# Layer 1 of a four-layer graph kernel: one fp32r product of 256 columns for two weights, and a new order of the work around it

## The chip, the cores and the metric

The kernel runs on one core of a Trainium2 chip. The core has five engines with queues of their own: TensorE (PE; its weight loads are shown as PEld), VectorE (DVE), ScalarE (ACT), GpSimd (POOL) and SyncE (SP), which here only issues DMAs. The metric is device time in microseconds of one execution; it stands at 913.17 us before the change, the median of 3 runs (912.57 to 913.24).

## The reference, cut to what matters

Four residual layers work on x, 32 samples of 512 tokens with 128 features, and share one 512 x 512 matrix adj. The change lies in layer 1, a Chebyshev graph convolution of order 2 whose two matrices are both adj:

```python
# h = max(layernorm(x), 0); A1 = A2 = adj
hops(h, A) = [h A, 2 (h A) A - h]          # A acts on the token axis
xs  = [h] + hops(h, adj) + hops(h, adj)
out = relu(concat(xs) @ Theta1 + bias)     # Theta1: 5 blocks of 128 x 128
x   = x + out
```

Since both matrices are adj, the five blocks of Theta1 fold into three: th[0] = T0 - T2 - T4 for h itself (the "own part"), th[1] = T1 + T3 for one hop, th[2] = 2 (T2 + T4) for two hops. With x1 = adj applied to h, the layer is h th[0] + adj (h th[1] + x1 th[2]) + bias, and then relu and the residual sum.

## The kernel before

All of x stays in SBUF. xt[q] holds a pair q of samples (q = 0 to 15, b = 0 or 1 in it), xq[r] a quadruple r (0 to 7). TensorE, DVE, ACT and POOL execute in the order of the source (manual_schedule, line 182), so the Python order of the calls is each engine's queue. SP is not in that list: its DMAs are placed by the framework, except where keep_in_program_order holds them.

Products with adj use three fp32r products instead of an fp32 one: an operand is split in parts high, low and mid (moving_parts, line 418: high on ACT, low on POOL, mid on DVE), and the three partial products with the parts of adj add up in one PSUM bank. Projections with the small weights are plain fp32 products of 128 columns (projected, line 442). A sample has four token tiles (NT = 4).

Layer 1 (layer1, line 950) runs a loop over r with the pairs A = 2r and C = 2r + 1. For each pair:

- normalised (line 956) makes h with eight ACT rows; turn (line 964) transposes it in 32 x 32 blocks on DVE and sends it through DRAM (four writes, then one read, on SP), so that h comes back with its features on the partitions, as hT.
- straighten (line 971) copies hT into the token order, hs, on POOL, two copies for a pair.
- split_up (line 976) splits a sample's h in its three parts; first (line 981, with mixed_parts, line 400) makes x1 transposed: 12 fp32r products of 512 columns, with one eviction on ACT (line 407).
- weighed (line 986) makes w = h th[1] + x1 th[2] in one bank, 8 fp32 products of 128 columns, and evicts it in three parts (lines 992 to 994: high on ACT, low and mid on DVE).
- mix (line 996) is called four times for a quadruple, one token tile i of all four samples each: four fp32 products of the own part, hs with th[0] (line 999), then 12 fp32r products of 512 columns with adj and w (line 1003). DVE then adds the bias and takes relu plus residual (lines 1005 and 1007).

In the loop, the mixing of quadruple r - 1 comes early in round r, between the preparations of pairs A and C. ln_stats and own take the layer-norm statistics of finished pairs for the next layer (four DVE rows, one ACT square root, two short DVE rows). The generator square, advanced by go(square, ...), prepares the square of adj for layer 2 on POOL, one step at a time in rounds 3 to 6. In the last round, more(0) to more(7) (line 1358) start layer 2.

The tiles that matter: small_tile, 13 of 128 x 512 (parts of h, x1, features); wide_tile, 6; the pool tag hT, 4 (hT and hs of pairs); 8 PSUM banks. A tile is taken again only after its last reader.

The weights of layer 1 are combined on POOL late in layer 0 (late_parts, line 733); line 744 scales th[0] by 1/UP, since mixing multiplies the whole bank by UP afterwards.

Of the kernel before, what the change touches and what calls it, by code (L numbers as in the profile page):

```python
# [9 lines left out]
F32 = mybir.dt.float32  # L10
# [4 lines left out]
OP = mybir.AluOpType  # L15
# [14 lines left out]
def kernel(  # L30
# [56 lines left out]
    def tiles(ap):  # L87
        return ap.rearrange("p (t f) -> p t f", f=D)

    def blk(t):  # L90
        return slice(t * P, (t + 1) * P)
# [56 lines left out]
    def spread(w, n):  # L148
        return w[:, None, :].to_broadcast([P, n, D])
# [250 lines left out]
    def mixed_parts(name, left, right, dst):  # L400

        p = bank(f"p_{name}")
        for part in range(3):
            for t in range(NT):
                nc.tensor.matmul(p, right[part][:, blk(t)], left[part][:, t, :],  # L405
                                 start=(t == 0 and part == 0), stop=(t == NT - 1 and part == 2))
        nc.scalar.activation(dst, p, AF.Copy, scale=UP)  # L407

    def three(name):
        return [small_tile(f"{part}_{name}", F32R) for part in PARTS]  # L410
# [7 lines left out]
    def moving_parts(x, high, low, mid):  # L418

        nc.scalar.activation(high, x, AF.Copy, scale=DOWN)  # L420
        nc.gpsimd.tensor_sub(low, x, high.bitcast(F32))  # L421
        nc.vector.scalar_tensor_tensor(mid, x, 1.0 / UP, high.bitcast(F32), OP.mult, OP.subtract)  # L422

    def scaled_parts(x_low, high, low, mid):

# [13 lines left out]
    def columns(xT):  # L439
        return lambda t: xT[:, blk(t)]  # L440

    def projected(name, *terms):

        p = bank(name)
        for t in range(NT):
            for i, (hT, w) in enumerate(terms):
                nc.tensor.matmul(p[:, blk(t)], hT(t), w, start=(i == 0),  # L447
                                 stop=(i == len(terms) - 1))
        return tiles(p)
# [283 lines left out]
    def late_parts():  # L733

        adj_parts.extend(matrix_tile(f"adj_{part}", F32R) for part in PARTS[:2])
        high, low = adj_parts
        for t in range(NT):
            nc.scalar.activation(high[:, t, :], adj_s[:, t, :], AF.Copy, scale=DOWN)
            tc.keep_in_program_order(nc.gpsimd.tensor_sub(adj_s[:, t, :], adj_s[:, t, :], high[:, t, :].bitcast(F32)))
            yield  # L740
        for out, op, p, q in ((1, OP.add, 1, 3), (2, OP.add, 2, 4), (0, OP.subtract, 0, 2)):
            tc.keep_in_program_order(nc.gpsimd.tensor_tensor(th[:, out, :], th[:, p, :], th[:, q, :], op))
        tc.keep_in_program_order(nc.gpsimd.tensor_scalar(th[:, 2, :], th[:, 2, :], 2.0, None, OP.mult))
        nc.gpsimd.tensor_scalar(th[:, 0, :], th[:, 0, :], 1.0 / UP, None, OP.mult)
        for t in range(NT):
            nc.scalar.activation(low[:, t, :], adj_s[:, t, :], AF.Copy, scale=LOW)
        yield
        adj_parts.append(matrix_tile(f"adj_{PARTS[2]}", F32R))
        for t in range(NT):
            tc.keep_in_program_order(nc.gpsimd.tensor_sub(adj_parts[2][:, t, :], high[:, t, :].bitcast(F32),  # L750
                                                          low[:, t, :].bitcast(F32)))
            yield
# [197 lines left out]
    def layer1(more, square):  # L950


        h, hT, hs, parts, x1, w = {}, {}, {}, {}, {}, {}
        normal, turning = {}, {}

        def normalised(q, n=2 * NT):
            if q >= NQ:
                return
            if q not in normal:
                h[q] = normed_tile(q)  # L960
                normal[q] = normed_steps(q, h[q])
            go(normal[q], n)

        def turn(q, n=3):
            if q >= NQ:
                return
            if q not in turning:
                turning[q] = turn_steps(h[q], f"hT1_{q}", hT)
            go(turning[q], n)

        def straighten(q):
            hs[q] = work.tile([P, 2, N], F32, tag="hT", name=f"hs_{q}", bufs=4)
            for b in range(2):
                nc.gpsimd.tensor_copy(split(hs[q][:, b]), hT[f"hT1_{q}"][:, :, b, :].rearrange("p b (a c) -> p a b c", c=QR))  # L974

        def split_up(q, b):
            if q < NQ:
                parts[q, b] = three(f"h_{q}_{b}")
                moving_parts(h[q][:, b].rearrange("p t f -> p (t f)"), *parts[q, b])

        def first(q, b):
            if q < NQ:
                x1[q, b] = small_tile(f"x1T_{q}_{b}")
                mixed_parts(f"x1T_{q}_{b}", adj_parts, parts[q, b], x1[q, b])

        def weighed(q, b):
            r, j = q // 2, 2 * (q % 2) + b
            if j == 0:
                w[r] = [wide_tile(f"w_{part}_{r}", F32R) for part in PARTS]
            p = projected(f"p_w_{q}_{b}", (columns(hs[q][:, b]), th[:, 1, :]), (columns(x1[q, b]), th[:, 2, :]))  # L990
            high, low, mid = (part.rearrange("p t (w f) -> p t w f", f=D)[:, :, j, :] for part in w[r])
            nc.scalar.activation(high, p, AF.Copy, scale=DOWN)
            nc.vector.tensor_sub(low, p, high.bitcast(F32))
            nc.vector.scalar_tensor_tensor(mid, p, 1.0 / UP, high.bitcast(F32), OP.mult, OP.subtract)

        def mix(r, i):
            p = bank(f"p_l1_{r}_{i}")
            for j in range(4):
                nc.tensor.matmul(p[:, blk(j)], columns(hs[2 * r + j // 2][:, j % 2])(i), th[:, 0, :],  # L999
                                 start=(j == 0), stop=False, skip_group_check=True)  # L1000
            for part in range(3):
                for t in range(NT):
                    nc.tensor.matmul(p, adj_parts[part][:, t, blk(i)], w[r][part][:, t, :],  # L1003
                                     start=False, stop=(part == 2 and t == NT - 1), skip_group_check=True)
            nc.vector.scalar_tensor_tensor(tiles(p), tiles(p), UP, spread(b1, 4), OP.mult, OP.add)
            x = xq[r].rearrange("p w b t f -> p (w b) t f")[:, :, i, :]
            nc.vector.scalar_tensor_tensor(x, tiles(p), 0.0, x, OP.max, OP.add)

        normalised(0)
        yield  # L1010
        turn(0)
        normalised(1)
        yield
        split_up(0, 0)
        split_up(0, 1)
        first(0, 0)
        straighten(0)
        turn(1)
        for r in range(NQ // 2):
            A, C = 2 * r, 2 * r + 1  # L1020
            last = r == NQ // 2 - 1
            if r == 0:
                first(A, 1)
                split_up(C, 0)
                split_up(C, 1)
                straighten(C)
            else:
                split_up(A, 1)
                straighten(A)
                mix(r - 1, 0)  # L1030
                normalised(C, NT)
                turn(C, 1)
                mix(r - 1, 1)
                normalised(C)
                turn(C)
                mix(r - 1, 2)
                split_up(C, 0)
                go(square, r > 3)
                mix(r - 1, 3)
                split_up(C, 1)  # L1040
                first(A, 1)
            weighed(A, 0)
            weighed(A, 1)
            if last:
                more(0)
            go(square, r > 2)
            first(C, 0)
            normalised(A + 2, NT)
            if last:
                more(1)  # L1050
            if r:
                ln_stats(A - 2)
            else:
                go(own[NQ - 3])
                go(own[NQ - 2])
            first(C, 1)
            if last:
                more(2)
            if r:
                straighten(C)  # L1060
            split_up(A + 2, 0)
            normalised(A + 2)
            go(square, r > 3)
            weighed(C, 0)
            weighed(C, 1)
            ln_stats(C - 2) if r else go(own[NQ - 1])
            go(square, r > 3)
            turn(A + 2)
            first(A + 2, 0)
            if r == 0:  # L1070
                normalised(C + 2, 0)
        more(3)
        for i in range(NT):
            mix(r, i)
            more(4 + i)
        yield
# [177 lines left out]
    def layers_2_and_3():  # L1254
# [15 lines left out]
        for n in range(B):  # L1270
# [16 lines left out]
                fetch(2, 2)  # L1287
            elif n % 2 and n + 5 < B:
                fetch(2, n // 2 + 3)
            if n in (2, 3):  # L1290
                ln_stats(NQ - 4 + n)
            if n == 12:
                weights_of_3()
            if n == 20:
# [135 lines left out]
```

## Time and profile before

| what | us |
|---|---|
| median of 3 runs | 913.17 |
| lowest, highest | 912.57, 913.24 |
| the profiled execution, its own time | 912.96 |
| its span on the core | 911.2 |
| layer 1 on TensorE, first product with adj to last mixing | 183.6 to 450.6 |

The page gives, for each engine, busy time and share of the span. A group line gives source line, engine, operation, output and inputs, shape, count, then the busy time in us with the mean of one row in ns, and the idle time before these rows with what ended it. A timeline line gives start, length, engine, line, operation and count; neighbouring rows of one kind are merged, so that its length runs from the first start to the last end. The chain of waits is followed back from the last instruction; in order of time, each piece is given with its start and length. In the view of stretches, each engine's busy time is followed by its number of rows, and the last three columns are TensorE's granted clock, the share of the DMA engines and their GB/s.

An fp32 product leaves two matmul records, an fp32r product one.

### The profile page before, as it was taken

The numbers are of one execution on the slowest core, as the hardware profiler recorded it, in microseconds if no ns is written. First come the engines' busy times: TensorE is split into PE (matmuls) and PEld (weight loads), VectorE is DVE, ScalarE is ACT, GpSimd is POOL, SyncE is SP. The second block draws the span as 40 slices with busy tenths as digits, with TensorE's granted clock in tenths as the row PEclk, the third lists the DMA queues.
The fourth block names the chain that finished last, engine by engine and source line by source line (L and its number), as shares of the span: only waits on it lengthen the run. The fifth ranks groups of instructions, "written<-read, shape, count | busy, mean of one in ns | idle before, by whom it ended". The sixth has DMA issues, their size and how long they took to land.

```text
span 911.2 us, 15170 instructions
## 1 busy us (share of the span) xinstructions
PE 901.1 (99%) x5432; PEld 774.2 (85%) x5433; DVE 669.7 (74%) x1348; ACT 527.5 (58%) x1156; POOL 485.6 (53%) x435
## 2 busy tenths in 40 slices
PE   8999999999999999999999999999999999999998
PEld 4899999988888888888877777777789999999998
DVE  7888886566656665665767777777698888987775
ACT  5874554343532442452556768876577767666663
POOL 5867999932132163342254445545475555666553
PEclk9999999999999999999999999999999999999999
DMA  9255644123114313212332344455212223222111
GB/s 265 50 167 165 186 122 118 24 71 93 35 59 119 87 31 90 71 46 76 106 120 70 93 126 129 132 147 160 70 48 82 81 82 91 73 70 81 59 36 47
DMA packets 83915, 86.06 MB, mean 94 GB/s; under 512 B 6784, under 2 KB 74624, under 8 KB 83840
## 3 DMA queue, kind: packets, MB, share of 16 engines
q1 hardware_dynamic: 83552, 84.57, 32.8%
q8 instruction: 43, 0.70, 0.3%
q10 hardware_dynamic: 288, 0.52, 0.2%
q14 instruction: 32, 0.26, 0.1%
HBM read 44.17 MB, written 40.89 MB: 93 GB/s over the span
## 4 chain that ended last, share of the span: by engine, by line
PE 92%; ACT 3%; DVE 3%; POOL 1%; issue 0%; DMA 0%; DVEq 0%; POOLq 0%; ACTq 0%
PE p_av L1234 12%; PE p_l L1003 10%; PE p_x1T L405 9%; PE p_score L1212 9%; PE p_msgT L1142 9%; PE p_w L447 6%; PE p_l_c L393 4%; PE p_l L999 3%; PE p_l_a L393 3%; PE p_l_d L393 3%; PE p_g L447 3%; PE p_l L447 3%; PE p_hv L447 3%; PE p_feat L447 3%; PE p_phi L1151 3%; PE p_phi L1152 3%
## 5 line engine op out<-in xcount | busy, mean ns | idle before, releaser
L1234 PEld LDWEIGHTS p_av<-hv,ex 128*128 128x128 f32 x1024 | 119.3, 191 | 3.7 <-POOL ex L1207 1.0
L1234 PE MATMUL p_av<-hv,ex 128*128 128x129 f32 x1024 | 119.8, 274 | 0.8 <-POOL ex L1207 0.8
L421 POOL TENSOR_TENSOR low_feat<-feat,high_feat 128x512 fp32r<-128x512 f32 x32 | 53.9, 1686 | 115.8 <-ACT high_feat L420 111.7
L285 ACT ACTIVATE h<-x,sh,rs 128x128 f32<-128x128 f32 x256 | 102.8, 483 | 11.8 <-DVE sh L257 11.0
L1207 DVE TENSOR_TENSOR ex<-ex,adjTx 128x512 f32<-128x512 f32 x64 | 80.4, 1259 | 35.7 <-ACT ex L1205 34.0
L1207 POOL TENSOR_TENSOR ex<-ex,adjTx 128x512 f32<-128x512 f32 x64 | 98.1, 1551 | 12.2 <-ACT ex L1205 8.1
L1093 ACT ACTIVATE h<-x,sh,rs 128x128 f32<-128x128 f32 x256 | 102.9, 485 | 0.0
L428 POOL TENSOR_TENSOR key<-key 128x512 fp32r<-128x512 f32 x32 | 50.2, 1567 | 97.9 <-DVE key L427 39.8
L421 POOL TENSOR_TENSOR low_h<-h,high_h 128x512 fp32r<-128x512 f32 x32 | 47.1, 1482 | 76.6 <-ACT high_h L420 76.4
L245 DVE BATCH_NORM_STATS2 bn<-x 128x6 f32<-128x256 f32 x244 | 85.9, 417 | 0.0
L407 ACT ACTIVATE x1T<-p_x1T 128x512 f32<-128x512 f32 x32 | 19.0, 594 | 109.4 <-PE p_x1T L405 100.8
L1205 ACT ACTIVATE ex<-ex 128x512 f32<-128x512 f32 x128 | 78.9, 651 | 0.0
L1213 ACT ACTIVATE ex<-p_score 128x512 f32<-128x512 f32 x128 | 74.0, 604 | 1.4 <-PE p_score L1212 1.1
L974 POOL COPY hs<-hT 128x512 f32<-128x512 f32 x32 | 18.6, 612 | 81.5 <-DMA hT<-d_hT 81.3
L432 ACT ACTIVATE high_query<-p_query 128x512 fp32r<-128x512 f32 x32 | 19.2, 599 | 73.8 <-PE p_query L1185 73.8
L422 DVE SCALAR_TENSOR_TENSOR mid_feat<-feat,high_feat 128x512 fp32r<-128x512 f32 x32 | 28.9, 904 | 44.3 <-ACT high_feat L420 44.3
L1212 PE MATMUL p_score<-high_query,key 128*128 128x512 f32 x128 | 50.5, 394 | 0.0
L1212 PE MATMUL p_score<-low_query,key 128*128 128x512 f32 x128 | 50.3, 393 | 0.0
L1212 PE MATMUL p_score<-mid_query,key 128*128 128x512 f32 x128 | 50.3, 393 | 0.0
L447 PE MATMUL p_w<-th,x1T 128*128 128x128 f32 x256 | 49.6, 275 | 0.3 <-ACT x1T L407 0.3
L254 ACT ACTIVATE sd<-bn,eps 128x8 f32<-128x8 f32 x46 | 13.9, 302 | 61.5 <-DVE bn L245 57.4
L447 PE MATMUL p_w<-th,hs 128*128 128x128 f32 x256 | 49.4, 275 | 0.0
(220 smaller groups left out, 2350.4 us busy)
## 6 DMA issues: line engine op xcount, KB each, us to landing
d<-hb SPq DMA_DIRECT2D x128, 128.0 KB, 2.5
hT<-d SPq DMA_DIRECT2D x32, 512.0 KB, 3.4
d_hT<-hb_hT SPq DMA_DIRECT2D x112, 128.0 KB, 2.4
hT<-d_hT SPq DMA_DIRECT2D x28, 512.0 KB, 3.3
x<-in_x_dram SPq DMA_DIRECT2D x32, 256.0 KB, 5.0
out_dram<-x SPq DMA_DIRECT2D x31, 256.0 KB, 2.3
adjT_d<-adj_squares SPq DMA_DIRECT2D x4, 256.0 KB
adj_crossed<-in_adj_dram SPq DMA_DIRECT2D x4, 256.0 KB
```

The costliest lines, as they stand in the source:

```text
L245: nc.vector.bn_stats(st[:, k].rearrange("p e s -> p (e s)"), xt[q][:, b, t : t + 2, :].rearrange("p t f -> p f t"))
L285: nc.scalar.activation(h[:, b, t, :], xt[q][:, b, t, :], AF.Relu, bias=shift[q][:, i : i + 1], scale=scale[q][:, i : i + 1])
L393: nc.tensor.matmul(p[:, i * 2 * D : (i + 1) * 2 * D], a[:, k, blk(i)], b[:, k], start=(first and i == 0 and k == 0), stop=(k == 1), skip_g ...
L405: nc.tensor.matmul(p, right[part][:, blk(t)], left[part][:, t, :], start=(t == 0 and part == 0), stop=(t == NT - 1 and part == 2))
L421: nc.gpsimd.tensor_sub(low, x, high.bitcast(F32))
L447: nc.tensor.matmul(p[:, blk(t)], hT(t), w, start=(i == 0), stop=(i == len(terms) - 1))
L1003: nc.tensor.matmul(p, adj_parts[part][:, t, blk(i)], w[r][part][:, t, :], start=False, stop=(part == 2 and t == NT - 1), skip_group_check= ...
L1093: nc.scalar.activation(h[:, t, :], xt[q][:, b, t, :], AF.Relu, bias=shift[q][:, i : i + 1], scale=scale[q][:, i : i + 1])
L1142: nc.tensor.matmul(p, feats[n][part][:, blk(t)], sq[part][:, t, :], start=(t == 0 and part == 0), stop=(t == NT - 1 and part == 2))
L1207: eng.tensor_mul(split(ex[:, t, :]), split(ex[:, t, :]), crossed(mask[:, t, :]))
L1212: nc.tensor.matmul(p, keys[n][i][:, t, :], query[n][i], start=(i == 0), stop=(i == 2))
L1234: nc.tensor.matmul(po[:, i, : D + 1], ex[:, t, blk(i0 + i)], hv[:, t, :], start=(t == 0), stop=(t == NT - 1))
```

## The change

The own part leaves mix. The turned h is now split in three parts as well (split_turned), and so are th[0] and th[1] side by side (fixed_parts, once). weighed multiplies each token tile with both weights at once, three fp32r products of 256 columns, into [own | w] in PSUM, and adds x1 th[2] to the w half with an fp32 product as before. Two banks are used for a sample. From each, ACT takes the high part of w and then the own part, which goes back into hs; DVE makes low and mid of w; POOL adds the bias to the own part. mix has its 12 fp32r products alone, and DVE adds the own part from hs in two rows for a tile instead of the bias in one.

The scale of x1's eviction (UP) and line 744 go. Ahead of the loop, the four first products of pairs 0 and 1 are called before any weighed. In the loop, turned h is split ahead of its product, the statistics go through stats_steps in three portions and start with r = 2 (four pairs fall to layer 2, n = 2 to 5, where it was two), turn and straighten move, and normalised of the next pair A stands between the mixing steps.

```diff
     def mixed_parts(name, left, right, dst):
...
-        nc.scalar.activation(dst, p, AF.Copy, scale=UP)
+        nc.scalar.copy(dst, p)
...
+    def fixed_parts(x, high, low, mid):
+
+        nc.scalar.activation(high, x, AF.Copy, scale=DOWN)
+        nc.gpsimd.tensor_sub(x, x, high.bitcast(F32))
+        nc.scalar.activation(low, x, AF.Copy, scale=LOW)
+        nc.gpsimd.tensor_sub(mid, high.bitcast(F32), low.bitcast(F32))
...
-        nc.gpsimd.tensor_scalar(th[:, 0, :], th[:, 0, :], 1.0 / UP, None, OP.mult)
...
+        def split_turned(q, b):
+            hs_parts[q, b] = three(f"hs_{q}_{b}")
+            moving_parts(hs[q][:, b], *hs_parts[q, b])
+
...
         def weighed(q, b):
...
-            p = projected(f"p_w_{q}_{b}", (columns(hs[q][:, b]), th[:, 1, :]), (columns(x1[q, b]), th[:, 2, :]))
-            high, low, mid = (part.rearrange("p t (w f) -> p t w f", f=D)[:, :, j, :] for part in w[r])
-            nc.scalar.activation(high, p, AF.Copy, scale=DOWN)
-            nc.vector.tensor_sub(low, p, high.bitcast(F32))
-            nc.vector.scalar_tensor_tensor(mid, p, 1.0 / UP, high.bitcast(F32), OP.mult, OP.subtract)
+            ps = [bank(f"p_w_{q}_{b}_{i}") for i in range(2)]
+            for t in range(NT):
+                p = ps[t // 2][:, t % 2 * 2 * D : (t % 2 + 1) * 2 * D]
+                for part in range(3):
+                    nc.tensor.matmul(p, hs_parts[q, b][part][:, blk(t)], th_parts[part],
+                                     start=(part == 0 and t % 2 == 0), stop=False, skip_group_check=True)
+                nc.tensor.matmul(p[:, D:], x1[q, b][:, blk(t)], th[:, 2, :], start=False, stop=True,
+                                 skip_group_check=True)
+            for i, p in enumerate(ps):
+                p = p.rearrange("p (t k f) -> p k t f", t=2, k=2)
+                high, low, mid = (part.rearrange("p t (w f) -> p t w f", f=D)[:, 2 * i : 2 * i + 2, j, :]
+                                  for part in w[r])
+                nc.scalar.activation(high, p[:, 1], AF.Copy, scale=UP * DOWN)
+                nc.scalar.activation(tiles(hs[q][:, b])[:, 2 * i : 2 * i + 2, :], p[:, 0], AF.Copy, scale=UP)
+                nc.vector.scalar_tensor_tensor(low, p[:, 1], UP, high.bitcast(F32), OP.mult, OP.subtract)
+                nc.vector.tensor_sub(mid, p[:, 1], high.bitcast(F32))
+            nc.gpsimd.tensor_add(tiles(hs[q][:, b]), tiles(hs[q][:, b]), spread(b1, NT))
 
         def mix(r, i):
             p = bank(f"p_l1_{r}_{i}")
-            for j in range(4):
-                nc.tensor.matmul(p[:, blk(j)], columns(hs[2 * r + j // 2][:, j % 2])(i), th[:, 0, :],
-                                 start=(j == 0), stop=False, skip_group_check=True)
             for part in range(3):
                 for t in range(NT):
                     nc.tensor.matmul(p, adj_parts[part][:, t, blk(i)], w[r][part][:, t, :],
-                                     start=False, stop=(part == 2 and t == NT - 1), skip_group_check=True)
-            nc.vector.scalar_tensor_tensor(tiles(p), tiles(p), UP, spread(b1, 4), OP.mult, OP.add)
+                                     start=(part == 0 and t == 0), stop=(part == 2 and t == NT - 1))
+            for k in range(2):
+                pk = tiles(p)[:, 2 * k : 2 * k + 2, :]
+                nc.vector.scalar_tensor_tensor(pk, pk, UP, hs[2 * r + k][:, :, blk(i)], OP.mult, OP.add)
...
         split_up(0, 0)
         split_up(0, 1)
         first(0, 0)
+        turn(1)
+        split_up(1, 0)
+        first(0, 1)
+        pair = small_tile("th_high", F32R), small_tile("th_low", F32R)
+        th_parts = pair[0][:, : 2 * D], pair[0][:, 2 * D :], pair[1][:, : 2 * D]
+        fixed_parts(th[:, 0:2, :].rearrange("p k f -> p (k f)"), *th_parts)
+        split_up(1, 1)
         straighten(0)
-        turn(1)
+        first(1, 0)
+        split_turned(0, 0)
+        first(1, 1)
+        split_turned(0, 1)
+        normalised(2)
+        straighten(1)
```

The loop's order after the change, in one list (before, it is lines 1019 to 1071):

```python
early, late_stats = ((stats_steps(q) if r > 1 else iter(())) for q in (A - 4, C - 4))
if r:
    split_up(A, 1); straighten(A); mix(r - 1, 0)
    normalised(C, NT); turn(C, 1); mix(r - 1, 1)
    go(early, NT); normalised(C); turn(C); split_turned(A, 0); mix(r - 1, 2)
    split_turned(A, 1); go(early, 1); go(square, r > 3); normalised(A + 2); mix(r - 1, 3)
    go(early); first(A, 1); split_up(C, 0); straighten(C)
weighed(A, 0)
if r: split_up(C, 1)
weighed(A, 1)
if last: more(0)
split_turned(C, 0); go(square, r > 2)
if r: first(C, 0)
go(late_stats, NT)
if last: more(1)
split_turned(C, 1); turn(A + 2, 1)
if r: first(C, 1)
go(late_stats, 1)
if last: more(2)
split_up(A + 2, 0); turn(A + 2); go(square, r > 3)
weighed(C, 0); weighed(C, 1); go(late_stats); go(square, r > 3)
first(A + 2, 0)
if r == 0: normalised(C + 2, 0), then the three remaining own statistics
```

More of the change, by code (lines that the diff above doesn't have):

```diff
@@ L950, in layer1 @@
     def layer1(more, square):
[L953 removed]
+        h, hT, hs, parts, hs_parts, x1, w = {}, {}, {}, {}, {}, {}, {}
         normal, turning = {}, {}
@@ L1021, in layer1 @@
             last = r == NQ // 2 - 1
[L1022 to L1027, printed above, removed]
+            early, late_stats = ((stats_steps(q) if r > 1 else iter(())) for q in (A - 4, C - 4))
+            if r:
                 split_up(A, 1)
@@ L1033, in layer1 @@
                 mix(r - 1, 1)
+                go(early, NT)
                 normalised(C)
                 turn(C)
+                split_turned(A, 0)
                 mix(r - 1, 2)
+                split_turned(A, 1)
+                go(early, 1)
+                go(square, r > 3)
+                normalised(A + 2)
+                mix(r - 1, 3)
+                go(early)
+                first(A, 1)
                 split_up(C, 0)
-                go(square, r > 3)
-                mix(r - 1, 3)
+                straighten(C)
+            weighed(A, 0)
+            if r:
                 split_up(C, 1)
-                first(A, 1)
-            weighed(A, 0)
             weighed(A, 1)
@@ L1045, in layer1 @@
                 more(0)
+            split_turned(C, 0)
             go(square, r > 2)
-            first(C, 0)
-            normalised(A + 2, NT)
+            if r:
+                first(C, 0)
+            go(late_stats, NT)
             if last:
                 more(1)
+            split_turned(C, 1)
+            turn(A + 2, 1)
             if r:
[L1052 to L1056, printed above, removed]
+                first(C, 1)
+            go(late_stats, 1)
             if last:
                 more(2)
-            if r:
-                straighten(C)
             split_up(A + 2, 0)
-            normalised(A + 2)
+            turn(A + 2)
             go(square, r > 3)
@@ L1065, in layer1 @@
             weighed(C, 1)
-            ln_stats(C - 2) if r else go(own[NQ - 1])
+            go(late_stats)
             go(square, r > 3)
-            turn(A + 2)
             first(A + 2, 0)
@@ L1071, in layer1 @@
                 normalised(C + 2, 0)
+                for q in (NQ - 3, NQ - 2, NQ - 1):
+                    go(own[q])
         more(3)
@@ L1289, in layers_2_and_3 @@
                 fetch(2, n // 2 + 3)
-            if n in (2, 3):
-                ln_stats(NQ - 4 + n)
+            if n in (2, 3, 4, 5):
+                ln_stats(NQ - 6 + n)
             if n == 12:
```

## The prediction

> **What bounds the kernel now.** I read the page's engine totals first, then the chain of waits, then the chain in order of time inside layer 1, then busy time by stretch, last single rows. The totals and the chain's shares:
>
> ```profile
> PE 901.1 (99%) x5432; PEld 774.2 (85%) x5433; DVE 669.7 (74%) x1348; ACT 527.5 (58%) x1156; POOL 485.6 (53%) x435
> ...
> PE 92%; ACT 3%; DVE 3%; POOL 1%; issue 0%; DMA 0%; DVEq 0%; POOLq 0%; ACTq 0%
> ```
>
> TensorE never rests, so a change pays what it takes from TensorE's list and loses every hole that it opens. One sample of layer 1 in the chain in order of time (start, length, count):
>
> ```profile
> 220.25 2.78 PE p_x1T L405 x12
> 223.03 3.57 PE p_w L447 x32
> ...
> 235.73 2.80 PE p_x1T L405 x12
> 238.53 0.89 PE p_l L999 x8
> 239.42 2.80 PE p_l L1003 x12
> ```
>
> Read per sample: x1T 2.79, its weights half of 3.57 = 1.785, own part 0.89, mixing 2.80, in all 8.265 us. Times four it is 33.06, and first products of successive rounds start 33.06 apart (235.49, 268.55, 301.62): no hole in rounds 1 to 7. An fp32 product of 128 columns leaves two records, 3.57/32 = 0.1116 us each, 0.223 together; an fp32r product of 512 columns leaves one, 2.79/12 = 0.232.
>
> Busy time of two rounds, without and with more of the adjacency square (columns: length, then PE, PEld, DVE, ACT, POOL):
>
> ```profile
> 301.60:334.70 33.10, 33.10 (x196) 28.80 (x194) 20.42 (x37) 13.29 (x30) 12.19 (x13) 1.00 0.24 65
> 334.70:367.70 33.00, 33.00 (x194) 28.72 (x193) 20.04 (x37) 13.30 (x30) 15.33 (x17) 1.00 0.24 64
> ```
>
> The helpers have room. What the new operations resemble:
>
> ```profile
> L457 POOL TENSOR_TENSOR x<-x,b 128x512 f32<-128x512 f32 x8 | 10.3, 1286 | 0.0
> L342 ACT COPY attT<-p_attT 128x256 f32<-128x256 f32 x6 | 2.0, 366 | 1.0 <-DVE sums_att L357 0.5 <-PE p_attT L487 0.5
> L357 DVE TENSOR_TENSOR sums_att<-p_attT,attT 128x256 f32<-128x256 f32 x2 | 0.7, 416 | 0.0
> ...
> 299.48 0.69 DVE L422 SCALAR_TENSOR_TENSOR mid_h<-h,high_h 128x512 fp32r<-128x512 f32 x1 [1.16 <-ACT high_h L420]
> 299.53 1.80 POOL L421 TENSOR_TENSOR low_h<-h,high_h 128x512 fp32r<-128x512 f32 x1 [7.95 <-ACT high_h L420]
> 306.81 1.30 POOL L421 TENSOR_TENSOR low_h<-h,high_h 128x512 fp32r<-128x512 f32 x1 [5.48 <-ACT high_h L420]
> 307.35 1.31 DVE L422 SCALAR_TENSOR_TENSOR mid_h<-h,high_h 128x512 fp32r<-128x512 f32 x1
> ```
>
> The last four: whichever of mid (DVE) and low (POOL) starts second grows from 0.69 or 1.30 by some 0.5. So the two do not add freely.
>
> [...] 0.223/128 = 1.74 ns a column against 0.232/512 = 0.45. [...]
>
> **The change part by part.**
>
> *TensorE.* Per sample 24 fp32 records go (16 of weights, 8 of own part) = 2.675 us. There come 12 fp32r products of 256 columns, a width that the trace does not have in fp32r, and 8 fp32 records (x1T by the third weight) = 0.89. [...] I take 125[...]. Four changes from fp32 to fp32r per sample cost some 0.01 each (in 200 to 235 us, one such change makes four products 0.95 to 1.0 instead of 0.93). New weights: 12 x 0.125 + 0.89 + 0.04 = 2.43. Per sample 8.01 instead of 8.265: 0.255 x 32 = **8.2 us saved**. At 116 it is 11.7, at 139 3.0; break-even lies near 0.146.
>
> *Helpers, per sample.* ACT: one split (0.62) and three more 256-wide evictions, some 0.85 net. DVE: a third split row (0.69 to 1.31), and the two 0.69 rows of the eviction in four of about 0.42; each mixing step one more 0.42. POOL: low of the turned h, 1.30 to 1.80, and the bias sum, 1.29: 2.8 x 4 = 11.2 a round, so 12 becomes 23 and, with the square, 15 becomes 26 to 28 of 32. These lie beside TensorE unless a deadline falls.
>
> *Steady round, deadlines from the start of weighed(A,0).* TensorE: two weighed to 4.86, two first products to 10.42, weighed(C,0) at 10.42, (C,1) at 12.85. POOL's list from there, in source order: low of C,0 may start at 1.45 (x1T eviction 0.2 to 0.8, high to 1.4) and runs to 3.2 beside DVE's mid; straighten(C) to 4.4; bias sum to 6.2; low of C,1 to 7.5 (wanted at 8.6, good); bias sum to 9.3; low of turned C,0 to 10.65[...]. Wanted at 10.55: 0.1 late, x 7 rounds = 0.7. [...] In rounds 4 and 5 a square step (1.26 + 0.62, with losses 1.95) stands between that and low of turned C,1: 14.4 instead of 12.5, wanted at 13.1: 1.3 late, x 2 = 2.6. Steady loss **3.3**. ACT (13.3 + 4 x 1.47 = 19 of 32) and DVE (20.4 + 4 x 1.4 = 26) keep their deadlines.
>
> *The start.* Before, there is 0.3 of waiting. Now the order f00, f01, f10, f11, w00, w01, w10, w11 runs on TensorE without other work. (1) ACT waits in the split of theta for POOL's subtraction (0.75), so high of h(1,1) comes at 192.2 and its low at 193.7 to 194: first(1,1) from 192.05 loses 0.9. (2) straighten(0) now stands behind that low on POOL; turned (0,0) is split by 197, the product wants it at 195.9: 1.0. (3) weighed(0,1) ends near 201.6 and weighed(1,0) follows at once, but the split of turned (1,0) stands on ACT behind all evictions of weighed(0,1), and its low on POOL behind the bias sum: 0.2 drain, about 0.65 + 0.65 of evictions (ACT comes late from eight normalising rows, 3.2), high 0.6, bias sum and low 1.3 + 1.3: ready near 205.9, 4.3 lost. Start: **6.2 lost**, bounds 4.5 and 8 (a halved clock after (3) would be the upper one).
>
> *Free edits.* The scale moved out of the x1T eviction leaves 0.59. Statistics in steps are the same rows; four sets go to the first layer-2 samples, where DVE has 2 us more at n = 4 and 5, as at 2 and 3 before, under 6.3 us of TensorE per sample. Thirteen small tiles less two for theta: each split takes the slots that the product just before it frees, and ACT is behind that product anyway. Two banks for p_w: five of eight in use. The last round's turned halves for layer 2 arrive 1.3 us before features(2) wants them instead of 2.2.
>
> Sum against the profiled run's own 912.96 (span 911.2): -8.2 + 6.2 + 3.3 = +1.3, **914.3 us**, 1.1 above the median of 913.17.
>
> **The rivals.** (B) *The holes stay small and the narrow product is cheap.* 116 ns, [...]the start loses 5: -11.7 + 5 = **906.3**. For it: POOL holds 12 of 33 now, mid rows can wait. Against: point (3) follows from program order alone. (C) *Turned h arrives late.* SP's order is not the source's:
>
> ```profile
> 307.45 6.99 SPq L328 DMA_DIRECT2D d_hT<-hb_hT  x5
> 314.66 0.34 SPq L330 DMA_DIRECT2D hT<-d_hT  x1
> 319.26 1.17 POOL L974 COPY hs<-hT 128x512 f32<-128x512 f32 x2 [11.15 <-DMA hT<-d_hT]
> ```
>
> A fifth write, of the next pair, stands ahead of the read of this pair, which waits for it. Before, only a copy hung on it; now the split does, on ACT ahead of eight normalising rows. If the read stays behind that write (at about 24.5 of the round, landed at 28), ACT comes 1.3 late to the next round, and POOL's list with it: 7 x 1.3 = 9.1, **923.4**, slower. It decides once turned h lands after 27. Against: the transposes now come some 4 us earlier, 10 us ahead of the next pair's. (D) *The 256-wide product does not run at the wide ones' rate*: 139 gives -3.0 + 6.2 + 1.8 = **918**; at fp32's rate (0.43 each) it would be over 100 us and the change would not do what it says, 2 in 100.
>
> **How the numbers follow.** My forecast 46 in 100, its own range 909 to 919; B 28, C 12, D 14. 0.2% (1.8 us) is about what a measurement of this kernel tells from no change. The forecast's own spread splits 30/20/50 into faster, same, slower; B is faster nearly always, C and D slower: faster 0.41, same 0.12, slower 0.47. Leaving one in ten at each end gives 905 to 921.
>
> **What would show it.** In the profile after: a hole of some 4 us on TensorE between the second and third weighed near 202 us, ended by low (POOL) or high (ACT) of hs; fp32r records of 256 columns 125 ns apart; rounds of 32.1 us, 33.4 in the two with the square; POOL 23 to 28 busy per round. Wrong if the start has no hole over 2 us, if those products are 112 or 140 apart, or if rounds keep waiting for hT.

## The result, and the profile after

The changed kernel took 917.39 us, the median of 5 runs (916.10 to 917.76), against 912.98 (912.57 to 913.24, 5 runs) before: a ratio of 1.0045, 95% interval 1.0030 to 1.0060. It is slower by 4.4 us. The profiled execution took 917.76 with a span of 916.0, 4.8 more than before's 912.96 and 911.2. In layer 1, from the first product with adj to the first product of layer 2, it is 4.06 of these: 183.77 to 454.80, against 183.61 to 450.58. The rest of the program grew by 0.7.

The engine totals and the chain's shares of the page after:

```profile
PE 896.2 (98%) x5305; PEld 764.6 (83%) x5305; DVE 708.8 (77%) x1476; ACT 569.6 (62%) x1286; POOL 579.9 (63%) x500
...
PE 83%; DVE 5%; ACT 4%; POOL 4%; DMA 2%; issue 2%; SPq 0%; DVEq 0%; POOLq 0%; ACTq 0%
```

TensorE is busy for 4.9 us less, and the program is 4.8 longer: it stands idle for 9.7 us more. (What a slower clock adds is counted as busy time: 4.00 of the 4.00 us from 208 on, at a granted clock of 0.55.) POOL grew by 94 us, from 485.6 to 579.9. The chain leaves TensorE in 17% of the span where it was 8%.

The same sample as before in the chain in order of time (start, length, what, count), two first products and the third weighed and mixing that follow, in a round without holes:

```profile
267.97 5.58 PE p_x1T L405 x24
273.55 0.38 PE p_w L1006 x3
273.93 0.22 PE p_w L1008 x2
274.15 0.36 PE p_w L1006 x3
274.51 0.22 PE p_w L1008 x2
...
278.20 2.80 PE p_x1T L405 x12
281.00 5.13 PE p_l L1024 x22
```

One token tile is three fp32r products of 256 columns, 0.36, and an fp32 product in two records, 0.22. Four tiles are 2.32, with 2.79 for the first product and 2.80 for mixing 7.91 a sample, or 31.65 a round: the distance of rounds 2, 3 and 6 (277.96 to 309.63, for example), where before it was 33.06. So TensorE's own gain is 1.41 a round, 11.3 over eight.

What took it back begins with the start. Timeline of the kernel after, 194 to 207 us; the bracket is the engine's idle time before the row and what ended it:

```profile
194.31 1.20 PE L405 MATMUL p_x1T<-adj_low,low_h 128*128 128x512 f32 x4 [0.77 <-POOL low_h L421]
197.40 0.38 PE L1006 MATMUL p_w<-th_high,low_hs 128*128 128x256 f32 x1 [0.84 <-POOL low_hs L421]
197.49 3.18 ACT L285 ACTIVATE h<-x,sh,rs 128x128 f32<-128x128 f32 x8
201.88 2.51 POOL L1018 TENSOR_TENSOR hs<-hs,b 128x512 f32<-128x512 f32 x2 [1.31 <-ACT hs L1015]
202.74 1.15 ACT L420 ACTIVATE high_hs<-hs 128x512 fp32r<-128x512 f32 x2
203.42 0.39 PE L1006 MATMUL p_w<-th_high,high_hs 128*128 128x256 f32 x1 [1.27 <-ACT high_hs L420]
204.33 3.41 POOL L421 TENSOR_TENSOR low_hs<-hs,high_hs 128x512 fp32r<-128x512 f32 x2
206.12 0.58 PE L1006 MATMUL p_w<-th_high,low_hs 128*128 128x256 f32 x1 [2.31 <-POOL low_hs L421]
206.49 0.41 PE L1006 MATMUL p_w<-th_low,mid_hs 128*128 128x256 f32 x1
```

All three holes stand here in their order, the third in two parts (1.27 and 2.31), with the cause of the third beside it: ACT makes eight normalising rows and the evictions before it reaches high of hs, and POOL makes two bias sums (2.51) before it reaches low. The last line shows something more: 0.41 for a row that is 0.28 elsewhere. The view of stretches has the reason; the third column from the end is the granted clock:

```profile
200.00:204.00 4.00, 2.54 (x20) 2.15 (x18) 2.75 (x9) 4.00 (x13) 2.69 (x4) 1.00 0.01 2
204.00:208.00 4.00, 1.89 (x9) 1.89 (x10) 4.00 (x4) 0.41 (x1) 4.00 (x4) 0.60 0.01 4
208.00:212.00 4.00, 4.00 (x23) 4.00 (x22) 2.41 (x6) 1.32 (x4) 2.07 (x2) 0.55 0.50 127
```

The granted clock is 0.50 from 204.79 to 211.62. From 206.1 to 211.4 the products run at half rate, 0.21 apart in place of 0.12. The two weighed from 206.12 to 213.15 take 7.03; at full rate they would take 4.5 (eight tiles of 0.58, less the product already done). The slow clock cost 2.5 us.

The steady rounds lose in three places: round 1 (33.16 long), round 4 (34.20) and round 5 (33.41), against 31.65: 1.5 + 2.55 + 1.75 = 5.8. The last round adds a hole of 0.6 before layer 2, which waits for its turned halves (one row of SP ahead of that read took 2.1 us to issue; the reason is not known). POOL's rows in rounds 1, 4 and 5, in the timeline of the kernel after:

```profile
234.19 1.63 POOL L980 COPY hs<-hT 128x512 f32<-128x512 f32 x2 [1.51 <-DMA hT<-d_hT]
...
330.73 1.32 POOL L980 COPY hs<-hT 128x512 f32<-128x512 f32 x2 [1.07 <-DMA hT<-d_hT]
...
337.90 1.29 POOL L1387 TENSOR_TENSOR adj_crossed<-adj_crossed,sq_high 128x512 f32<-128x512 f32 x1
...
369.60 1.30 POOL L421 TENSOR_TENSOR low_hs<-hs,high_hs 128x512 fp32r<-128x512 f32 x1
370.85 1.75 POOL L1387 TENSOR_TENSOR adj_crossed<-adj_crossed,sq_high 128x512 f32<-128x512 f32 x1
372.69 0.94 POOL L1388 TENSOR_SCALAR sq_low<-adj_crossed 128x512 fp32r<-128x512 f32 x1
373.70 1.27 POOL L421 TENSOR_TENSOR low_hs<-hs,high_hs 128x512 fp32r<-128x512 f32 x1
```

In round 5 the square's two rows stand between the two low parts; the second is done at 374.97, and TensorE had stood idle for 1.49 by then. In round 1 it is straighten that waits for its DMA. Round 4 has both, straighten's wait of 1.07 and the square's step, and two holes (0.68 and 1.05).

The account of layer 1: -11.3 (rate), +8.5 (round 0 took 29.38 up to the next quadruple's first product where its products alone are 20.4, and 0.5 of such excess was there before), +5.8, +0.9 (the last hole, priced as below): 3.9 of the measured 4.06. Of the 8.5, the holes show 4.9 net of before's 0.3, the clock is 2.5, and the remaining 1.1 lies around the holes: a row's end is 0.16 past the start of its successor in a full line, and the row after a hole takes 0.1 more, so that a hole costs some 0.25 more than its bracket says.

### The profile page after: what moved, and what is told of

It is laid out like the page before. It is cut to its first block, busy times and chain, and to the rows that moved or that the text cites. A ratio compares the mean times of both kernels' runs of the same rounds, so it can differ in the third digit from the quotient of the medians.

```text
span 916.0 us, 15448 instructions
## 1 busy us (share of the span) xinstructions
PE 896.2 (98%) x5305; PEld 764.6 (83%) x5305; DVE 708.8 (77%) x1476; ACT 569.6 (62%) x1286; POOL 579.9 (63%) x500
## 4 chain that ended last, share of the span: by engine, by line
PE 83%; DVE 5%; ACT 4%; POOL 4%; DMA 2%; issue 2%; SPq 0%; DVEq 0%; POOLq 0%; ACTq 0%
PE p_av L1273 12%; PE p_score L1251 9%; PE p_l L1024 9%; PE p_msgT L1181 8%; PE p_x1T L405 7%; PE p_l_c L393 4%; PE p_w L1006 4%; PE p_l_a L393 3%; PE p_l_d L393 3%; PE p_g L454 3%; PE p_hv L454 3%; PE p_l L454 3%; PE p_feat L454 2%; PE p_w L1008 2%; PE p_query L1224 2%; PE p_phi L1190 2%
## 5 line engine op out<-in xcount | busy, mean ns | idle before, releaser
L421 POOL TENSOR_TENSOR low_feat<-feat,high_feat 128x512 fp32r<-128x512 f32 x32 | 56.1, 1755 | 101.7 <-ACT high_feat L420 101.7
L421 POOL TENSOR_TENSOR low_h<-h,high_h 128x512 fp32r<-128x512 f32 x32 | 50.4, 1577 | 60.1 <-PE p_w L1008 40.4
L422 DVE SCALAR_TENSOR_TENSOR mid_feat<-feat,high_feat 128x512 fp32r<-128x512 f32 x32 | 24.4, 762 | 44.3 <-ACT high_feat L420 44.3
L407 ACT COPY x1T<-p_x1T 128x512 f32<-128x512 f32 x32 | 18.8, 587 | 63.0 <-PE p_x1T L405 62.7
L1018 POOL TENSOR_TENSOR hs<-hs,b 128x512 f32<-128x512 f32 x32 | 44.3, 1387 | 12.8 <-ACT hs L1015 6.0
L421 POOL TENSOR_TENSOR low_hs<-hs,high_hs 128x512 fp32r<-128x512 f32 x32 | 45.4, 1435 | 3.7 <-ACT high_hs L420 3.0
```

## The experiments

Each is the changed kernel with one edit, unless it says otherwise; ratios are against the kernel before.

**1. Bias sums late.** Theory: POOL's four bias sums a round, of 1.29 and more each, stand ahead of the low parts that TensorE waits for, and nobody needs them before mixing.

```diff
+        def biased_own(q, b):
             nc.gpsimd.tensor_add(tiles(hs[q][:, b]), tiles(hs[q][:, b]), spread(b1, NT))
...
             weighed(C, 1)
+            for q, b in ((A, 0), (A, 1), (C, 0), (C, 1)):
+                biased_own(q, b)
```

> The changed kernel with one edit: POOL's bias sums of a round (four of 1.3 us) are issued together after weighed(C,1) instead of one after each weighed. Theory (POOL's list decides the holes in layer 1): the low rows of h(C,1), turned (C,0) and turned (C,1) come 1.3 to 2.6 us earlier; the holes of rounds 1, 4 and 5 (about 1.4, 2.4 and 1.7 us beyond the usual spacing) close nearly, the second part of the hole at 203 us shrinks by 0.9; 5 to 6.5 us less than the changed kernel's 917.4, so 911 to 912.5, or 908.5 if TensorE's clock then isn't halved after the hole. Rival (the holes are set by late DMAs of turned h and by ACT): within 1 us of 917.4.

Measured 909.14 us (907.38 to 909.87), ratio 0.9955 [0.9940, 0.9970]: 8.2 less than the changed kernel, and faster than before. Rounds 1 to 6 are all 31.6 long. The timeline of this kernel in round 4:

```profile
326.71 1.48 POOL L980 COPY hs<-hT 128x512 f32<-128x512 f32 x2 [0.91 <-DMA hT<-d_hT]
...
331.11 1.29 POOL L1390 TENSOR_TENSOR adj_crossed<-adj_crossed,sq_high 128x512 f32<-128x512 f32 x1
332.48 0.94 POOL L1391 TENSOR_SCALAR sq_low<-adj_crossed 128x512 fp32r<-128x512 f32 x1
333.51 1.29 POOL L421 TENSOR_TENSOR low_hs<-hs,high_hs 128x512 fp32r<-128x512 f32 x1
...
338.29 5.50 POOL L1019 TENSOR_TENSOR hs<-hs,b 128x512 f32<-128x512 f32 x4
```

The square's rows still stand ahead of the second low part, and straighten still waits for its DMA, here 0.91; neither opens a hole any more, since the four sums (5.50) are behind them. So neither the square nor the DMA was the cause by itself: POOL's list was too long by the bias sums. At the start the hole before the low part falls from 2.31 to 0.97, yet the clock still drops in the profile (0.69 and 0.88 in the two stretches). The one of the four runs whose mean clock was 1.000 took 907.38, the two with 0.996 took 909.51 and 909.87.

**2. A filler in the hole.** To price the clock apart from the hole: sixteen fp32r products of 512 columns, whose result nobody reads, between the second and third weighed of round 0.

```diff
+            if r == 0:
+                p = bank("p_idle")
+                for _ in range(16):
+                    nc.tensor.matmul(p, adj_parts[0][:, 0, blk(0)], adj_parts[0][:, 0, :], start=True, stop=True)
```

> The changed kernel with 16 extra products (fp32r, 512 columns, 0.232 us each, into a bank that nobody reads) on TensorE between weighed(0,1) and weighed(1,0), where the hole of 3.6 us lies. Theory (the hole[...] halves TensorE's clock for some 5 us afterwards, which costs 2.5 us by itself): the clock stays at 1.0 between 204 and 212 us, the products of 256 columns there run 0.117 apart instead of 0.21, and the time falls by 2.5 us to 914.9. Rival (the slow stretch has another cause, such as contention from the DMAs then in flight): 917.4 or up to 0.5 more.

Measured 914.59 (914.03 to 916.52, 15 runs), ratio 1.0018 [1.0010, 1.0026], 2.8 less than the changed kernel. The stretches of this kernel (its trace holds no record of the clock, and the view then gives 1.00; the rate is read from the rows, 32 of them in the second stretch where the changed kernel has 23):

```profile
204.00:208.00 4.00, 3.74 (x25) 3.15 (x24) 4.00 (x4) 0.89 (x3) 4.00 (x4) 1.00 0.00 0
208.00:212.00 4.00, 4.00 (x32) 3.79 (x32) 3.38 (x9) 2.18 (x7) 3.00 (x3) 1.00 0.48 123
```

The wait for the parts is as long as it was, filled with useless work; in round 0 only the clock differs. Up to the next quadruple's first product the round takes 26.93 instead of 29.38: 2.45, the 2.5 read from the rows. (In the profiled execution round 4 is also 0.8 shorter, which has nothing to do with the filler.)

**3. The square's steps earlier.** From round 2 on two steps behind the third mixing step and one behind the next quadruple's first product, none between the low parts.

```diff
-                go(square, r > 3)
+                go(square, 2 * (r > 1))
...
-            go(square, r > 2)
...
-            go(square, r > 3)
...
+            go(square, r > 1)
```

> The changed kernel with the steps of the square of adj moved: from round 2 on, two a round while the quadruple before is mixed and one at the round's end, instead of one and three from round 4 on, of which one stands between the low rows of turned (C,0) and turned (C,1). Theory: the hole of round 5 (1.7 us) and the second hole of round 4 (1.3) close, the first of round 4 (0.8 and 0.3) stays since there turned h comes late from the DMA: 914.0 to 914.6. Rival [...]: 917, no change; if POOL becomes too full during the mixing, slower, 918 or more.

Measured 920.29 (919.62 to 920.50), ratio 1.0081 [1.0064, 1.0098]: slower. Rounds 4 and 5 went from 34.20 and 33.41 to 32.88 and 31.63, as the theory says (one hole of 0.67 stays in round 4), but the first step, one round earlier, needs a DMA of its own. Timeline of this kernel:

```profile
268.30 1.04 POOL L1382 TENSOR_TENSOR adj_crossed<-adj_crossed 128x512 f32<-128x512 f32 x1 [12.90 <-DMA adj_crossed<-in_adj_dram]
```

POOL stood for it with low of h behind it: a hole of 3.86 up to 271.4, and half the clock for 6.0 us after it. A step that is moved takes its DMA's landing time along; the expectation had left that out.

**4. The third split earlier.** Split of turned (C,0) ahead of the second weighed in round 0, so that its parts come before that one's evictions and bias sum.

```diff
+            else:
+                split_turned(C, 0)
             weighed(A, 1)
...
-            split_turned(C, 0)
+            if r:
+                split_turned(C, 0)
```

> The changed kernel with the split of turned (1,0) placed before weighed(0,1) in round 0, so that ACT does it ahead of the evictions of weighed(0,1) and POOL ahead of their second bias sum. Theory (the order of ACT's and POOL's lists makes the hole): the 3.8 us of the hole at 202 to 206 us fall to 1.5 or less, with a smaller new one before weighed(1,1), the clock stays at 1.0, and the time falls by 4 to 5 us, to 912.5 to 913.5. Rival (the split waits for tiles or for turned h itself): the hole stays, 917.

Measured 916.04 (915.09 to 920.12), ratio 1.0037 [1.0023, 1.0052], 1.35 less than the changed kernel where 4 to 5 were expected. Only the first part of the hole closed (1.27 to 0.14); the second stayed at 2.19. ACT's rows in this kernel say why:

```profile
198.73 3.18 ACT L285 ACTIVATE h<-x,sh,rs 128x128 f32<-128x128 f32 x8
201.81 0.36 ACT L1014 ACTIVATE w_high<-p_w 128x256 fp32r<-128x256 f32 x1
...
202.87 0.63 ACT L420 ACTIVATE high_hs<-hs 128x512 fp32r<-128x512 f32 x1
```

The eight normalising rows of the next quadruple stand ahead of everything; the split moved by one sample's evictions only.

**5. Start in another order.** Experiments 1 and 4 together, and the normalising of pair 2 behind the splits of pair 1.

```diff
-        normalised(2)
...
             split_turned(C, 1)
+            if r == 0:
+                normalised(2)
```

> e1_bias_late with two moves in round 0: the eight normalising rows of pair 2 come after both splits of turned pair 1 instead of ahead of the first weighed, and the split of turned (1,0) stands before weighed(0,1). Theory (the hole at 202 us is ACT's list: eight rows and two evictions ahead of the split): the 1.3 + 1.0 us of that hole shrink to 0.7 or less, no halved clock afterwards; 3 to 3.5 us below e1's 909.1, so 905.6 to 906.1. Rival (the low rows on POOL set the hole whatever ACT does): at most 1 us less than e1.

Measured 906.50 (905.91 to 907.96), ratio 0.9930 [0.9915, 0.9944], 2.6 less than experiment 1. The hole near 202 is down to 0.21 and 0.16, and the clock stays at 1.00 from 200 to 216 us. The four weighed still stand together here, so it is the order on ACT and POOL that opened this hole.

**6. Theta's split first.** Experiment 1, with the split of th[0] and th[1] ahead of the first product with adj.

```diff
+        fixed_parts(th[:, 0:2, :].rearrange("p k f -> p (k f)"), *th_parts)
         first(0, 0)
```

> e1_bias_late with the split of theta moved ahead of first(0,0), where ACT and POOL have free time. Theory (the holes at 193 and 196 us, some 0.9 and 1.0 beyond the usual spacing, come from ACT and POOL waiting for one another in that split): both close, 1.9 us less than e1's 909.1: 907.2. Rival (they come from hT or from the small tiles): no change, 909.

Measured 906.73 (905.92 to 907.30), ratio 0.9927 [0.9910, 0.9944], 2.4 less than experiment 1. The hole of 0.77 at 193 is gone and the one at 196 falls from 0.84 to 0.50; and though the holes near 202 are as long as in experiment 1, the clock stays at 1.00 in the profile from 200 to 216 us:

```profile
203.37 0.39 PE L1006 MATMUL p_w<-th_high,high_hs 128*128 128x256 f32 x1 [1.42 <-ACT high_hs L420]
204.72 0.38 PE L1006 MATMUL p_w<-th_high,low_hs 128*128 128x256 f32 x1 [0.97 <-POOL low_hs L421]
205.27 0.39 PE L1006 MATMUL p_w<-th_low,mid_hs 128*128 128x256 f32 x1 [0.16 <-DVE mid_hs L422]
```

Part of the 2.4 is therefore likely the clock: three of these four runs had a mean clock of 1.000, and only one of experiment 1's, which took 907.38.

**7. All three.** Experiments 1, 5 and 6 together.

> e1_bias_late with the moves of e5 and of e6 together. If both theories hold, layer 1 has no hole over 0.5 us left and the time is 909.1 - 3.3 - 1.9 = 903.9; if only one holds, 905.8 or 907.2.

Measured 904.80 (904.68 to 908.92), ratio 0.9920 [0.9898, 0.9941]. TensorE's idle time in layer 1 is 1.2 us in all, against 10.15 in the changed kernel. (The profiled execution is the longest, 908.92; its layer 1 began 4 us later than the changed kernel's, since in layer 0 a product waited 1.90 for its turned h, up to 68.8, and the clock was at half for 3.4 us behind it.)

**8. The width itself.** Each product of 256 columns as two of 128, all else the same.

> The changed kernel with each product of 256 columns made as two of 128, with the same operands and result; it measures what fp32r costs below 256 columns. If the price goes with the columns[...]: 0.058 apart, time near 917. [...] 1.3 us more per sample, up to 42 in all, 945 to 960. If narrow fp32r products fall to fp32's rate (0.22 for 128 columns): 4 us more per sample, 1030 to 1045.

Measured 956.1, one run, 38.7 more than the changed kernel. The clock was at half for 17 us of it, but its steady rounds, at full clock, take 36.63 against 31.65, 39.8 over eight. The chain in order of time of this kernel, with two tiles of the third weighed in round 3:

```profile
289.21 0.62 PE p_w L1007 x6
289.83 0.27 PE p_w L1011 x2
290.10 0.62 PE p_w L1007 x6
290.72 0.27 PE p_w L1011 x2
```

Six fp32r products of 128 columns and two fp32 records are 0.89, eight records of 0.111: an fp32r product of 128 columns takes what an fp32 record of 128 columns takes (0.112 before), the price behind the expectation's 945 to 960. The pair of weights in one product is the whole gain of the change: at 256 columns a product is 0.118, hardly dearer than at 128.

**9. Statistics in one go.** The prediction called their portions free; here they are undone.

```diff
-                go(early, NT)
...
-                go(early, 1)
...
-                go(early)
+                if r > 1:
+                    ln_stats(A - 4)
...
-            go(late_stats)
+            if r > 1:
+                ln_stats(C - 4)
```

> The changed kernel, with the layer-norm statistics of each finished pair taken in one go (for pair A - 4 behind the fourth mixing step, for pair C - 4 behind the second weighed of pair C) instead of in three portions; the same rows, none added. If the portions are free, as the prediction has it: 916.5 to 918, rounds 2 and 3 and 6 within 0.3 us of the changed kernel's 31.65. Rival: without the portions ScalarE's square root waits for four DVE rows just written and holds up the evictions behind it, and the DVE rows hold up low and mid of the weighed: a new hole of 0.5 to 1.5 us in each round from 2 on, 920 to 926.

Measured 920.24 (919.71 to 920.64), ratio 1.0079 [1.0064, 1.0094], 2.9 more than the changed kernel. Rounds 2 to 6 each have a hole of some 0.67 within the third weighed. Timeline of this kernel in round 2:

```profile
263.67 0.31 ACT L254 ACTIVATE sd<-bn,eps 128x8 f32<-128x8 f32 x1 [5.87 <-DVE bn L245]
263.88 0.57 ACT L407 COPY x1T<-p_x1T 128x512 f32<-128x512 f32 x1
264.35 0.63 ACT L420 ACTIVATE high_h<-h 128x512 fp32r<-128x512 f32 x1
265.06 1.80 POOL L421 TENSOR_TENSOR low_h<-h,high_h 128x512 fp32r<-128x512 f32 x1 [8.23 <-ACT high_h L420]
...
274.38 0.39 PE L1006 MATMUL p_w<-th_high,low_hs 128*128 128x256 f32 x1 [0.66 <-POOL low_hs L421]
```

ACT's square root waits for four DVE rows just made, the eviction and the split behind it come 0.5 late (264.35 for high of h, 263.85 in the changed kernel), POOL starts its list 0.5 later, and ten microseconds on TensorE waits 0.66 for the end of that list. The rival of this run held: the portions carry weight.

**10. Without the four first products up front.** Round 0 in the order of the steady rounds: two first products of pair 0, its two weighed, then pair 1.

```diff
-        split_up(1, 0)
-        first(0, 1)
...
-        first(1, 0)
...
-        first(1, 1)
-        split_turned(0, 1)
-        normalised(2)
-        straighten(1)
...
+            else:
+                first(A, 1)
+                split_turned(A, 1)
+                split_up(C, 0)
+                straighten(C)
             weighed(A, 0)
-            if r:
-                split_up(C, 1)
+            split_up(C, 1)
...
-            if r:
-                first(C, 0)
+            if r == 0:
+                normalised(2)
+            first(C, 0)
```

> The changed kernel without the four first products up front: round 0 takes the order of the steady rounds (two first products of pair 0, its two weighed, then first products and weighed of pair 1), all else as in the changed kernel. If the hole of 3.6 us near 202 us and the halved clock behind it come from the four weighed standing together: that hole is gone, the clock stays near 1.0, and what is left is a hole of 1 to 3 us before the first weighed, since turned h of pair 0 has two first products less to be split under; 912 to 914. Rival: the hole only moves ahead of the first weighed and is 4 us or more there, since the same splits must come before a product either way, and the clock drops with it; 917 or above.

Measured 910.87 (910.14 to 913.49, 20 runs), ratio 0.9983 [0.9976, 0.9989]: 6.5 less than the changed kernel, by this alone. The expectation was 912 to 914. In its timeline one hole of the start is left, of a length that was expected:

```profile
191.53 0.39 PE L1006 MATMUL p_w<-th_high,low_hs 128*128 128x256 f32 x1 [1.57 <-POOL low_hs L421]
```

Round 0 takes 22.78 up to the next quadruple's first product, against 29.38. Two first products (5.6 us) between two weighed and the next two give ACT and POOL time for the splits of pair 1. The clock shows in the time once more: 11 runs with a mean clock of 1.000 took 910.14 to 911.24, seven with 0.996 or 0.998 took 911.84 to 913.49. Where in the program it fell in those seven is not known, as the one profiled execution kept it; the kernel before had 0.998 in 4 of 23 runs as well.

**11. The best of it.** Experiment 10 with the bias sums late and theta's split first.

> Run e10's order of round 0, with the four bias sums of a round behind its last weighed (as in e1) and theta split ahead of the first product with adj (as in e6). If the causes are apart and add: holes of rounds 1, 4 and 5 gone (5 us or so), at most 2 us lost in round 0, 904 to 906. If what helped in e7 was only the longer way from split to product at the start, which this order gives up: 907 to 910.

Measured 903.57 (903.16 to 903.77), ratio 0.9896 [0.9881, 0.9911]. The totals of this kernel:

```profile
PE 891.3 (99%) x5304; PEld 762.3 (85%) x5305; DVE 703.8 (78%) x1476; ACT 569.5 (63%) x1286; POOL 582.1 (65%) x500
```

POOL does as much as in the changed kernel and TensorE's idle time in layer 1 is 0.5 us. This version beats both kernels, by 9.3 and 13.8 us.

## Why the prediction was right in sign, and where its terms were off

The forecast was 914.3, with 905 to 921 as its range and slower the likeliest of the three; it came out 3.1 higher, at 917.39. The sign was not a strong call: slower had 0.47 against 0.41 for faster, and the forecast change of +1.3 was less than the 1.8 that the prediction itself takes for the least that can be told from no change. That the total fell so near is in part luck, since a gain 3.1 larger than forecast stood against losses that were 5.7 larger (2.3 at the start, 2.5 in the rounds, 0.9 at the end).

*TensorE's gain* was the right mechanism with a term mis-sized: 8.2 forecast at 125 ns a product, 11.3 measured. (The forecast's own parts, 2.43 + 2.79 + 2.80, give 8.02 a sample and not 8.01, so 7.8 us in place of 8.2, and 11.3 and 2.5 at 116 and 139.) The 125 was the author's estimate, and so were 116 (half of the 232 that 512 columns take) and 139 (three fifths of it, if every product paid for 128 columns more). The chain after has 0.36 for three, some 0.12 each, which is near the 116; a weighed is 2.32, not 2.43. From 512 to 256 columns the measured price halves, 0.232 to 0.118.

*The start* was named hole by hole, with place and releaser, and the sizes were near: 0.77 for 0.9, 0.84 for 1.0, 3.58 for 4.3. The term that failed is the clock, which the sum left at zero and kept only as an upper bound of 8. It dropped to 0.50, and cost 2.5 (the rows; 2.45 by round 0 of experiment 2). With 1.1 around the holes, the start is 8.5 instead of 6.2.

*The steady rounds*: 3.3 forecast, 5.8 measured. The list on POOL, and the square's steps in it ahead of the second low part, are as described; rounds 4 and 5 lost 4.3 where 2.6 was forecast for the square, and a part of round 4's loss is straighten's wait of 1.07 for the turned h. The 0.1 a round for all others did not show in rounds 2, 3 and 6, and instead round 1 lost 1.5, since POOL's straighten waited 1.51 for the turned h, a wait that the list did not have. Experiment 1 shows that what made both expensive is the bias sums, which the prediction counted in the list but took as fixed in it: put last, they leave enough slack for the square and the late DMA.

*Rival C*, turned h late through SP's order, did not happen as told: in every round SP issued a pair's four writes and then its own read. Turned h did come late in rounds 1 and 4, by the 1.51 and 1.07 above; why the DMA was late there is open.

```profile
258.62 1.75 SPq L328 DMA_DIRECT2D d_hT<-hb_hT  x4
262.34 0.34 SPq L330 DMA_DIRECT2D hT<-d_hT  x1
```

These are SP's rows in round 2 of the kernel after. *Rival B* was right on the price of the narrow product, and wrong on the holes. *Rival D* fell with the width: its total, 918, is the nearest of the four to the measured one, but by luck, since its product of 139 ns measured 118.

*The free edits* were not all free of effect. The last round's hole of 0.6 is the slack of 1.3 for layer 2's turned halves, gone. And "statistics in steps are the same rows" was wrong as a reason for nothing: the rows are the same, but experiment 9 puts their order at 2.9 us in the changed kernel.

## What to carry to other kernels

When one engine gets more to do, look at its order before its total: POOL at 63% cost 5.8 us in three rounds through four additions that nobody needed until later, and none when these stood last. Operands made by helpers need a stretch of other TensorE work between their making and their use; four weighed placed together use up that stretch at once (experiment 10), unless the helpers take the splits ahead of their other work (experiment 5). And a hole is to be priced with the clock behind it: in the changed kernel half the clock around the hole of 2.31 cost 2.5 us more.

## What the hardware showed that was not expected

The clock fell around short holes. The longest was 2.31 us in the changed kernel, 2.19 in experiment 4 and 1.27 in experiment 1, and in each the products ran at half rate afterwards, for 5.3, 3.5 and 3.4 us.

The length of the holes alone does not tell whether it falls: experiments 1 and 6 have last holes that are alike, 1.27 and 0.97 against 1.42 and 0.97. The stretches of experiment 1 and then of experiment 6, with TensorE's busy time as the second figure:

```profile
200.00:204.00 4.00, 2.21 (x17) 1.82 (x16) 3.09 (x9) 4.00 (x12) 1.12 (x2) 1.00 0.01 2
204.00:208.00 4.00, 3.39 (x17) 3.19 (x18) 4.00 (x4) 0.74 (x3) 4.00 (x4) 0.69 0.02 4
208.00:212.00 4.00, 4.00 (x29) 3.83 (x29) 3.07 (x9) 1.98 (x6) 3.96 (x3) 0.88 0.50 127
...
200.00:204.00 4.00, 2.33 (x18) 1.94 (x17) 2.79 (x9) 4.00 (x13) 1.15 (x2) 1.00 0.01 2
204.00:208.00 4.00, 3.12 (x25) 2.92 (x25) 4.00 (x4) 1.37 (x5) 4.00 (x3) 1.00 0.02 4
208.00:212.00 4.00, 4.00 (x27) 3.61 (x26) 4.00 (x11) 1.61 (x6) 4.00 (x4) 1.00 0.43 110
```

TensorE is idle for 2.40 of the eight us up to 208 in experiment 1 and for 2.55 in experiment 6; the granted clock falls to 0.69 and 0.88 in the one and stays at 1.00 in the other. What parts them is not shown. In the changed kernel half the clock lasted 6.83 us (204.79 to 211.62), of which TensorE was still idle for 1.3, and in experiment 8 17 us; why it lasted so long there is open.

The price of an fp32r product went with its columns down to 256, 0.232 at 512 and 0.118 at 256, and then stopped: 0.111 at 128, as for an fp32 record of the same width. From 256 to 128 columns a narrower product gives next to nothing back here (no width between them was run), and a second small weight set beside the first costs 0.007.
